# The last image of a windowed-attention block and dynamic convolution: early mean and taps, rows exchanged by channel group, two convolution pieces on TensorE and one on three engines

## The chip, the cores and the metric

The kernel runs on one core of one Trainium2 chip, as one launch. A core has five engines with instruction streams of their own: TensorE (matmul, PE in the profile), VectorE (DVE), ScalarE (ACT), GpSimd (POOL) and SyncE (SP), which here only issues DMAs. They meet through semaphores, and each takes its own instructions strictly in order. The metric is the device time of one execution in microseconds, lower is better. The kernel before takes 2823.23 us (median of three runs, 2822.96 to 2826.73).

## The reference

The input is 16 images of 192 channels and 56 x 56 pixels, float32. Two layers follow each other.

The first is a shifted-window attention block: layer norm over the channels, attention in 7 x 7 windows (shift 3, 6 heads) with relative position bias, a projection, a residual, a second layer norm, a two-layer network 192-768-192 with gelu, and a residual.

The second is the layer that the change touches, a depthwise convolution whose weights depend on the image:

```python
pooled = x.mean(axis=(2, 3))
t = pooled @ w1.T
t = gamma * (t - running_mean) * rsqrt(running_var + EPS) + beta
t = relu(t)
wt = t @ w2.T + b2            # 9 weights per channel and image
wt = wt * MASK                # of the 3 x 3 taps only the first four are left
out = depthwise_conv(x, wt, padding=1) + bias
```

The four taps left are the three of the row above and the left neighbour in the same row. Nothing of an image's convolution can be computed before the mean over all of its pixels is known, and the mean needs the end of the first layer.

## The kernel before

**Tiling.** An image is cut into four units of 14 rows. 64 partitions hold the channels of one group (`g`, three groups of 64), and the two halves of the partitions (`P(0)`, `P(1)`) hold two halves of the image, 28 rows each (`LR`), of which a unit has seven (`WS`) in each half; a unit has 392 pixels (`UT`) per half. The image lives in `xt[b % 3]`, 128 partitions x 3 groups x 29 rows x 56; row 0 is a copy of the neighbouring half's last row (the "halo"), which the tap above needs. There are 64 units (`S`); each goes through attention, projection, first layer (`first_layer`, L799, six chunks `f` into `hid`, with gelu on ScalarE, L811) and second layer (`second_layer`). Four units stand at different stages at the same time.

**Second layer.** `second_layer` goes over the three channel groups; for each it multiplies the six chunks of `hid` (128 hidden units x 2 halves x 392) with `wf2` into one bank of PSUM (L837, 12 matmuls a group). Then `ends` (L824, VectorE) adds bias and residual, writes the pixels back into `xt` and leaves their sum in `sums`.

**Taps.** After the fourth unit `taps(b)` reduces `sums` (L859), multiplies with `w1t` (L867, 6 matmuls), scales, applies relu and multiplies with `w2r` (L879 to L897, VectorE) into `wt`, the four weights per channel. Then it sends the two halo rows of all groups with two DMAs from SyncE (L903).

**Convolution.** `conv(b, i)` computes one of six pieces: half of the rows of each half image (`hf`) by channel group (`g`); a piece has 128 partitions x 14 rows x 56. ScalarE takes the tap straight above with the bias (L929), VectorE adds the other three with one multiply-add each (L953), ScalarE sets one row of the second half's piece anew (L946: the image row 0, which has no row above), and SyncE stores the piece in two or three DMAs (L966). For the first 15 images the pieces go through the tiles `yt` and lie beside the attention of the next image. For the last image nothing follows: its results are written into `hid`, whose chunk `i` becomes free when the second layer has read it.

**Order.** The kernel writes every operation into a plan (`Plan.add`) with an engine, an estimated duration, what it reads and writes, a lag, and a `slack`: how long after its place in TensorE's order it is due. `Plan.order` then simulates the engines with these estimates: TensorE keeps the order in which operations were added; every other engine takes, among the operations that are ready first, the one due first. The instructions are issued in the order that comes out, and each engine then runs its own in that order. For the last image the order that comes out takes the six pieces tap by tap on VectorE: all first taps, then the others; SyncE's queue holds the two halo DMAs and then the 15 stores.

The main loop (`for r in range(-2, S + 3)`) adds the operations of all stages of a step `r`. At the last step, `r = S + 2`, only the second layer of the last unit, the taps and the six pieces are left.

Of the kernel before, what the change touches and what calls it, by code (L numbers as in the profile page):

```python
# [45 lines left out]
class Plan:  # L46
# [7 lines left out]
    def add(self, eng, dur, fn, reads=(), writes=(), lag=0.0, slack=60.0, by=None):  # L54
        i = len(self.ops)
        deps = set()
        reads, writes = flat(reads), flat(writes)
        for k in reads:
            if k in self.writer:
                deps.add(self.writer[k])  # L60
        for k in writes:
            if k in self.writer:
                deps.add(self.writer[k])
            deps.update(self.readers.get(k, ()))
        for k in reads:
            self.readers.setdefault(k, []).append(i)
        for k in writes:
            self.writer[k] = i
            self.readers[k] = []
        deps.discard(i)  # L70
        self.ops.append((eng, dur, fn, sorted(deps), lag, slack, by))
# [70 lines left out]
def tile_swin_then_dynamic_conv(  # L142
# [37 lines left out]
    def sb(name, *shape):  # L180
        return const.tile(list(shape), F32, tag=name, name=name)
# [40 lines left out]
    m2 = sb("m2", 128, HT)  # L222
    rs = sb("rs", 128, HT)
    sums = [sb(f"sums{i}", 128, G, NU) for i in range(2)]
    pooled = sb("pooled", 128, G)
    trow = sb("trow", 128, RED)
    prod = sq.rearrange("p g t -> p (g t)")[:, 0 : G * NTAP * RED]
# [32 lines left out]
    def X(s):  # L260

        b, u = divmod(s, NU)
        return [("x", b % 3, u, i) for i in range(3)]
# [550 lines left out]

            add("ACT", 0.95, go, [pk, "b1f", "table"], [("hid", f)])

    def second_layer(s):
        b, u = divmod(s, NU)
        xv = rows(s).rearrange("p g r c -> p g (r c)")
        for g in range(G):  # L820
            p, pk = bank()

            def ends(p=p, g=g):
                nc.vector.scalar_tensor_tensor(  # L824
                    xv[:, g],
                    p[:, 0, 0:UT],
                    vecs[:, 5, g : g + 1],
                    xv[:, g],
                    ALU.add,
                    ALU.add,  # L830
                    accum_out=sums[b % 2][:, g, u : u + 1],
                )

            for f in range(NFC):
                def product(p=p, g=g, f=f):
                    for ab in range(2):
                        nc.tensor.matmul(  # L837
                            p[P(ab), 0, 0:UT],
                            wf2[:, f, g * 64 : (g + 1) * 64],
                            hid[:, f, ab],  # L840
                            start=(f == 0),
                            stop=(f == NFC - 1),
                            tile_position=(0, 64 * ab),
                        )

                add("PE", 0.66, product, [("hid", f), ("wf2", f // 2)], [pk])
                if f == NFC - 1:
                    add("DVE", 0.65, ends, [pk, "vecs"], X(s) + [("sums", b % 2)])


    def taps(b):


        p, pk = bank()
        sl = b % 3
        add(
            "DVE",
            0.2,
            lambda: nc.vector.tensor_reduce(pooled, sums[b % 2], AX.X, ALU.add),  # L859
            [("sums", b % 2)],  # L860
            ["pooled"],
        )

        def product():
            for g in range(G):
                for ab in range(2):
                    nc.tensor.matmul(  # L867
                        p[P(ab), 0, 0:RED],
                        pooled[:, g : g + 1].broadcast_to([128, 64]),
                        w1t[:, g],  # L870
                        start=(g == 0),
                        stop=(g == G - 1),
                        tile_position=(0, 64 * ab),
                    )

        add("PE", 0.3, product, ["pooled", "w1t"], [pk])

        def scale():
            nc.vector.tensor_tensor(trow, p[:, 0, 0:RED], bns, ALU.mult)  # L879
            nc.vector.tensor_tensor(trow, trow, bnb, ALU.add)  # L880
            nc.vector.scalar_tensor_tensor(
                prod,
                trow.rearrange("p (o r) -> p o r", o=1).broadcast_to([128, G * NTAP, RED]),
                0.0,
                w2r.rearrange("p g t r -> p (g t) r"),
                ALU.max,
                ALU.mult,
            )

        add("DVE", 1.2, scale, [pk, "bn", "w2r"], ["sq", "trow"])  # L890
        w = wt[b % 2].rearrange("p g t -> p (g t)")

        def fin():
            nc.vector.tensor_reduce(
                w.rearrange("p (k o) -> p k o", o=1), prod, AX.X, ALU.add
            )
            nc.vector.tensor_tensor(w, w, b2t.rearrange("p g t -> p (g t)"), ALU.add)  # L897

        add("DVE", 0.9, fin, ["sq", "b2t"], [("wt", b % 2)])
        t = xt[sl]  # L900
        for to, of, row in ((0, 1, LR), (1, 0, LR)):
            def go(to=to, of=of, row=row):
                nc.sync.dma_start(t[P(to), :, 0, :], t[P(of), :, row, :])  # L903
            add("SP", 0.65, go, X(b * NU + NU - 1), [("halo", sl, to)], lag=2.5)

    pieces = [(hf, g) for hf in range(2) for g in range(G)]

    def conv(b, i):
        hf, g = pieces[i]
        sl = b % 3  # L910
        yi = (b * 6 + i) % 2
        y, yk = yt[yi], ("y", yi)
        if b == B - 1:

            y = hid[:, i].rearrange("p a (r c) -> p (a r) c", c=IMG)
            yk = ("hid", i)
        nr = LR // 2
        src = xt[sl][:, g]
        prev = src[:, nr * hf : nr * hf + nr]
        same = src[:, nr * hf + 1 : nr * hf + nr + 1]  # L920
        w = wt[b % 2]
        keys = [k for u in range(NU) for k in X(b * NU + u) if u // 2 == hf or u == 2 * hf - 1]
        if hf == 0:
            keys += [("halo", sl, 0), ("halo", sl, 1)]
        keys.append(("wt", b % 2))
        add(
            "ACT",
            1.05,
            lambda: nc.scalar.activation(  # L929
                y, prev, AF.Identity, bias=vecs[:, 6, g : g + 1], scale=w[:, g, 1:2]  # L930
            ),
            keys + ["vecs"],
            [yk],
        )
        for t, dst, s_ in (
            (0, y[:, :, 1:], prev[:, :, : IMG - 1]),
            (2, y[:, :, : IMG - 1], prev[:, :, 1:]),
            (3, y[:, :, 1:], same[:, :, : IMG - 1]),
        ):
            if t == 3 and hf == 1:  # L940

                r = IMG - SHIFT - LR - nr
                add(
                    "ACT",
                    0.35,
                    lambda: nc.scalar.activation(  # L946
                        y[64:128, r], zero[64:128], AF.Identity, bias=vecs[64:128, 6, g : g + 1]
                    ),
                    ["vecs", "zero"],
                    [yk],  # L950
                )
            def go(t=t, dst=dst, s_=s_):
                nc.vector.scalar_tensor_tensor(  # L953
                    dst, s_, w[:, g, t : t + 1], dst, ALU.mult, ALU.add
                )
            add("DVE", 1.4, go, keys, [yk])
        ch = slice(g * 64, g * 64 + 64)
        parts = [(0, 0, nr, SHIFT + nr * hf)]
        first = SHIFT + LR + nr * hf
        n = min(nr, IMG - first)  # L960
        parts.append((1, 0, n, first))
        if n < nr:
            parts.append((1, n, nr, 0))
        for h, lo, hi, at in parts:
            def go(h=h, lo=lo, hi=hi, at=at):
                nc.sync.dma_start(out[b, ch, at : at + hi - lo, :], y[P(h), lo:hi])  # L966
            add("SP", 0.65, go, [yk], [], lag=12.0)

    def table(name):
        add("ACT", 1.3, lambda: nc.scalar.preload_act_table_set(name), [], ["table"])  # L970
# [411 lines left out]
    for r in range(-2, S + 3):  # L1382
# [43 lines left out]
            fold_proj()  # L1426
        if has(r):
            turn_shares()
        if has(r - 3):
            second_layer(r - 3)  # L1430
        b, k = divmod(r - 3, NU)
        weighing = k == NU - 1 and 0 <= b < B
        if has(r - 1):
            biased_rows(r - 1)
            for _ in projection(r - 1):
                if weighing:
                    taps(b)
            statistics(1, r - 1)
        elif weighing:
            taps(b)  # L1440
        if not early and has(r + 1):
            queries_keys(r + 1, (0, 1, 2))
        if has(r - 2):
# [5 lines left out]
        for b in range(B):  # L1449
            k = r - (b * NU + NU + 3)  # L1450
            if b == B - 1 and r == S + 2:
                for i in range(6):
                    conv(b, i)
            elif b < B - 1 and 0 <= k < 3:
                conv(b, 2 * k)
                conv(b, 2 * k + 1)
# [80 lines left out]
```

## Time and profile before

| | us |
|---|---|
| median of three runs | 2823.23 |
| the profiled execution, its own time | 2820.61 |
| its span, first to last instruction | 2818.8 |
| TensorE busy | 2754.4 (98%) |
| VectorE busy | 1833.4 (65%) |
| ScalarE busy | 1671.2 (59%) |
| GpSimd busy | 1570.5 (56%) |
| end of TensorE's last layer | 2789.0 |
| end of VectorE's last multiply-add | 2811.1 |

The profile is one execution. Each row of its tables names a line, an engine, an operation and tiles (out<-in), the shape, how many there were, the time they were busy and the mean of one. Rows marked "q" (SPq, ACTq) are the engine's instruction queue, here the issuing of DMAs. A matmul in float32 shows as two records. A timeline row gives start and duration in microseconds from the start of the span. Rows of stretches give length, then busy time and number of instructions of TensorE, its weight loads, VectorE, ScalarE and GpSimd, then the granted clock of TensorE (1.00 is full), the DMA share and GB/s.

### The profile page before, as it was taken

How to read it: one execution, taken by the hardware profiler on the slowest of the kernel's cores; microseconds unless marked ns; L12 is line 12 of the kernel's file. 1: busy time of each engine (PE TensorE's matmuls, PEld its weight loads, DVE VectorE, ACT ScalarE, POOL GpSimd, SP SyncE). 2: the span in 40 equal slices, each digit the busy share in tenths (PEclk: the TensorE clock that was granted, in tenths of full speed). 3: DMA queues.
4: the chain of work that ended last, by engine and by line, in shares of the span. 5: the costliest groups of instructions: out<-in, count | busy, mean ns of one | idle time of the engine just before them, and what ended most of it. 6: DMA issues, size and time to landing. Idle time of an engine off the chain costs nothing.

```text
span 2818.8 us, 79628 instructions
## 1 busy us (share of the span) xinstructions
PE 2754.4 (98%) x34337; PEld 1716.8 (61%) x34337; DVE 1833.4 (65%) x3321; ACT 1671.2 (59%) x2530; POOL 1570.5 (56%) x1424
## 2 busy tenths in 40 slices
PE   7899999999999999999999999999999999999995
PEld 5566666666666666566566666566666666666652
DVE  6565676667576675766757676675766757666663
ACT  3656656556566566566556566565665666565552
POOL 5565564565565565564665555555655655655530
PEclk9899999999999999999999999999999999999998
DMA  6312232223314223232233313233142243312131
GB/s 130 80 28 48 64 89 49 67 63 79 79 43 105 42 62 85 54 89 59 61 69 79 78 43 89 41 79 79 43 105 55 50 85 74 84 44 65 31 76 39
DMA packets 122232, 189.35 MB, mean 67 GB/s; under 512 B 31208, under 2 KB 96664, under 8 KB 121880
## 3 DMA queue, kind: packets, MB, share of 16 engines
q1 hardware_dynamic: 117512, 184.24, 29.3%
q8 instruction: 270, 4.42, 0.7%
q10 hardware_dynamic: 4368, 0.02, 0.1%
q14 instruction: 82, 0.67, 0.1%
HBM read 66.81 MB, written 38.98 MB: 38 GB/s over the span
## 4 chain that ended last, share of the span: by engine, by line
PE 96%; DVE 1%; ACT 1%; POOL 1%; issue 1%; DMA 0%; ACTq 0%; SPq 0%; DVEq 0%; POOLq 0%
PE ps L837 27%; PE ps L799 27%; PE ps L469 14%; PE ps L654 9%; PE ps L760 5%; PE ps L690 5%; PE ps L549 5%; PE ps L746 3%; PE ps L318 2%; DVE hid L953 0%; POOL xs L425 0%; PE ps L867 0%; ACT o L717 0%; PE ps L383 0%; DVE trow L880 0%
## 5 line engine op out<-in xcount | busy, mean ns | idle before, releaser
L837 PE MATMUL ps<-hid,wf 128*64 128x392 f32 x4608 | 773.4, 494 | 3.3 <-issue 2.5
L799 PE MATMUL ps<-xs,wf 64*128 64x392 f32 x4608 | 769.5, 489 | 0.0
L799 PEld LDWEIGHTS ps<-xs,wf 64*128 64x128 f32 x4608 | 445.9, 187 | 312.5 <-issue 0.9
L837 PEld LDWEIGHTS ps<-hid,wf 128*64 128x64 f32 x4608 | 327.8, 137 | 413.8 <-issue 381.4
L302 POOL TENSOR_TENSOR fold<-sq 128x392 f32<-128x392 f32 x128 | 131.3, 1026 | 700.1 <-PE ps L318 693.6
L811 ACT ACTIVATE hid<-ps,b1f 128x784 f32<-128x784 f32 x384 | 343.0, 912 | 146.2 <-PE ps L799 143.4
L590 POOL TENSOR_TENSOR e<-e,top 128x784 f32<-128x784 f32 x192 | 285.6, 1503 | 253.8 <-DVE top L585 253.8
L469 PE MATMUL ps<-xs,wqkv 64*128 64x392 f32 x2304 | 408.5, 504 | 11.0 <-POOL xs L436 9.7
L953 DVE SCALAR_TENSOR_TENSOR y<-x,wt,y 128x770 f32<-128x770 f32 x270 | 302.8, 1136 | 85.7 <-ACT y L946 63.3
L469 PEld LDWEIGHTS ps<-xs,wqkv 64*128 64x128 f32 x2304 | 220.3, 190 | 178.1 <-issue 21.8
L608 POOL TENSOR_TENSOR e<-e,tot 128x784 f32<-128x784 f32 x192 | 290.6, 1524 | 56.8 <-DVE tot L603 54.7
L654 PE MATMUL ps<-wqkv,xs 64*64 64x192 f32 x6144 | 278.1, 325 | 0.6 <-issue 0.4
L454 POOL TENSOR_TENSOR xs<-x,rb 128x392 f32<-128x392 f32 x192 | 249.6, 1328 | 25.4 <-DMA rb<-rsd 25.4
L575 DVE TENSOR_TENSOR e<-ps,bt 128x784 f32<-128x784 f32 x192 | 175.3, 968 | 130.2 <-PE ps L549 130.2
L717 ACT COPY o<-ps 32x392 f32<-32x392 f32 x512 | 246.5, 481 | 8.7 <-PE ps L690 2.3
L619 DVE STREAM_TRANSPOSE tt<-e 128x512 f32<-128x512 f32 x384 | 246.2, 685 | 5.8 <-POOL e L608 4.3
L654 PEld LDWEIGHTS ps<-wqkv,xs 64*64 64x64 f32 x6144 | 224.6, 133 | 35.1 <-issue 22.1
L482 ACT ACTIVATE q<-ps,qbs 128x400 f32<-128x400 f32 (+1 forms) x128 | 68.4, 589 | 288.2 <-PE ps L469 288.2
L602 DVE TENSOR_REDUCE tot<-e 128x16 f32<-128x784 f32 x192 | 182.1, 948 | 63.2 <-ACT e L597 63.1
L339 DVE TENSOR_TENSOR m<-ps,m 128x196 f32<-128x196 f32 (+1 forms) x64 | 23.2, 362 | 306.4 <-ACT m L332 306.3
L728 ACT ACTIVATE x<-x,pbt 128x392 f32<-128x392 f32 x192 | 105.4, 612 | 191.2 <-POOL xs L436 191.2
L666 ACT COPY v<-ps 128x768 f32<-128x768 f32 x128 | 102.3, 799 | 194.3 <-PE ps L654 194.3
(106 smaller groups left out, 3548.5 us busy)
## 6 DMA issues: line engine op xcount, KB each, us to landing
pt<-tt SPq DMA_DIRECT2D x256, 192.0 KB
x<-in_x_dram SPq DMA_DIRECT2D x112, 294.0 KB
out_dram<-y SPq DMA_DIRECT2D x135, 196.0 KB
pt<-tt SPq DMA_DIRECT2D x256, 96.0 KB
rb<-rsd SPq DMA_DIRECT2D x118, 196.0 KB
out_dram<-y SPq DMA_DIRECT2D x45, 154.0 KB
x<-in_x_dram SPq DMA_DIRECT2D x16, 168.0 KB
pt<-tt SPq DMA_DIRECT2D x128, 12.0 KB
```

The costliest lines, as they stand in the source:

```text
L454: nc.gpsimd.tensor_tensor(xs2[:, g], xv[:, g], rb[:, 1], ALU.mult)
L469: nc.tensor.matmul(p[:, ab, 0:UT], lhs_qk(ab, g, i), d[P(ab), g, 0:UT], start=(g == 0), stop=(g == G - 1), tile_position=(64 * ab, 0),)
L590: nc.gpsimd.tensor_tensor(ev, ev, top[j].broadcast_to([128, 16, N]), ALU.subtract)
L602: nc.vector.tensor_reduce(tot[j], ev, AX.X, ALU.add)
L608: nc.gpsimd.tensor_tensor(ev, ev, tot[j].broadcast_to([128, 16, N]), ALU.mult)
L619: nc.vector.transpose(tt[:, kb, 16 * j : 16 * j + 16], src)
L654: nc.tensor.matmul(p[P(w % 2), ab, i * DIM : (i + 1) * DIM], d[P(ab), g, w * N : w * N + 64], wqkv[P(ab), g, 2 * DIM :], start=(g == 0), s ...
L717: add("ACT", 0.5, lambda dst=dst, src=src: nc.scalar.copy(dst, src), [k], [("o", j, i)])
L799: nc.tensor.matmul(p[:, ab, 0:UT], wf1[P(ab), g, f * 128 : (f + 1) * 128], xs2[P(ab), g], start=(g == 0), stop=(g == G - 1), tile_position ...
L811: nc.scalar.activation(hid[:, f], p[:, :, 0:UT], AF.Gelu, bias=b1f[:, f : f + 1])
L837: nc.tensor.matmul(p[P(ab), 0, 0:UT], wf2[:, f, g * 64 : (g + 1) * 64], hid[:, f, ab], start=(f == 0), stop=(f == NFC - 1), tile_position= ...
L953: nc.vector.scalar_tensor_tensor(dst, s_, w[:, g, t : t + 1], dst, ALU.mult, ALU.add)
```

## The change

For the 15 images before the last nothing is computed in another way; `taps` is cut into `mean`, `taps` and `halos`, and the row-0 operation and the stores of `conv` become functions of their own (`first_row`, `stores`). For the last image:

- `early_mean`: the sum of the last unit's pixels is built before the second layer ends: the residual's sum (`xsum`, a VectorE reduction of the rows) plus `wf2` times the sums of `hid` over the pixels (`hsum`, six VectorE reductions; 18 matmuls with one column) plus the bias. The 18 matmuls stand after group 0 of the second layer.
- `taps` of the last image stands in the middle of group 1 (`amid`, after chunk 2).
- `halos` sends the rows of groups 0 and 1 when group 1 has ended (`("fin", 1)`), and those of group 2 when it has ended; four DMAs instead of two.
- `conv_product`: pieces 4 (second rows, group 1) and 2 (first rows, group 2) are computed on TensorE. GpSimd scales an identity matrix (made in `q2`) with the tap weights of the channels, four 128 x 128 matrices in `q128` and `kbd`; 8 matmuls (two blocks of seven rows, four taps) add the taps in PSUM; ScalarE moves the result into `hid` with the bias (0.95 planned) and issues the stores from its own queue.
- Piece 0 is shared by three engines: ScalarE forms two of the products in `yt`, GpSimd adds them, VectorE has the last tap.
- Pieces 3, 5 and 1 stay on ScalarE and VectorE. The pieces wait for single groups (`("fin", g)`), not for all rows.
- Planned durations, lags and slacks of the last image's operations differ (0.95 instead of 1.4 for a multiply-add, lag 4 instead of 12 for a store, slack 50 and 52 instead of 60).

In the order that comes out, VectorE has after the weights: the end of group 1, one multiply-add of piece 3, the end of group 2, six multiply-adds of pieces 3, 1 and 5, a 64 x 55 correction for piece 4, two multiply-adds, and the last tap of piece 0. ScalarE has the straight taps of pieces 3, 1 and 5, a row, the straight tap and the first product of piece 0, the move of piece 4, two rows, the second product of piece 0, three stores, the move of piece 2 and two stores. GpSimd has the eight scalings, then the two additions. SyncE has ten stores.

```diff
-    def second_layer(s):
+    def second_layer(s, groups=range(G), amid=None):
...
+                if amid is not None and f == 2:
+                    amid()
                 if f == NFC - 1:
-                    add("DVE", 0.65, ends, [pk, "vecs"], X(s) + [("sums", b % 2)])
+                    add("DVE", 0.65, ends, [pk, "vecs"], X(s) + [("sums", b % 2), ("fin", g)])
...
+    def early_mean(b):
...
+        for f in range(NFC):
+            add("DVE", 0.85,
+                lambda f=f: nc.vector.tensor_reduce(
+                    hsum[:, f : f + 1], hid[:, f].rearrange("p a t -> p (a t)"), AX.X, ALU.add
+                ),
...
+        add("DVE", 1.3, lambda: nc.vector.tensor_reduce(xsum, xv, AX.X, ALU.add), X(s), ["xsum"])
...
+        def product():
+            for g in range(G):
+                for f in range(NFC):
+                    nc.tensor.matmul(
+                        p[0:64, 0, g : g + 1],
+                        wf2[:, f, g * 64 : (g + 1) * 64],
+                        hsum[:, f : f + 1],
...
+    def halos(b, gs=slice(0, G)):
...
+                nc.sync.dma_start(t[P(to), gs, 0, :], t[P(of), gs, row, :])
...
+                X(b * NU + NU - 1) if b < B - 1 else [("fin", gs.stop - 1)],
...
+    def conv_product(b, i, unit, uk, room, dk):
...
+        for t in range(NTAP):
+            add("POOL", 0.35,
+                lambda t=t: nc.gpsimd.tensor_scalar(
+                    diag[:, t], unit, w[:, g, t : t + 1], None, ALU.mult
+                ),
...
+            for j in range(2):
...
+                    nc.tensor.matmul(
+                        dst, diag[:, t], s_, start=(k == 0), stop=(k == NTAP - 1),
...
+        add("PE", 5.3, product, keys, [pk])
...
+        stores(b, hf, g, y, yk, "ACT", 3.0)
...
-            add("DVE", 1.4, go, keys, [yk])
+            if not room or t == 3:
+                add("DVE", 0.95 if b == B - 1 else 1.4, go, keys, [yk])
+                continue
...
+                nc.scalar.activation(part, s_, AF.Copy, scale=w[:, g, t : t + 1])
+            add("ACT", 1.05, go, keys, part_keys)
...
+                nc.gpsimd.tensor_tensor(dst, dst, part, ALU.add)
+            add("POOL", 2.1, go, part_keys, [yk])
...
+        if r == S + 2:
+            ahead = early_mean(B - 1)
+            next(ahead)
+            second_layer(S - 1, (0,))
+            for _ in ahead:
+                pass
+            second_layer(S - 1, (1,), lambda: taps(B - 1))
+            halos(B - 1, slice(0, 2))
+            second_layer(S - 1, (2,))
+            halos(B - 1, slice(2, 3))
...
-                for i in range(6):
+                unit = q2.rearrange("p w b c -> p (w b c)")[:, 0:128]
...
+                conv_product(b, 4, unit, uk, room, [("q128", h) for h in range(2)])
...
+                conv_product(b, 2, unit, uk, room, [("kbd", h) for h in range(2)])
+                conv(b, 0, [(yt[i], [("y", i)]) for i in range(2)])
+                for i in (3, 5, 1):
                     conv(b, i)
```

## The prediction

> **What bounds the kernel now.** I read the page's shares first (TensorE 98% of the span, the last of 40 slices at half), then the chain of waits, then the timeline of the last 45 us. Up to 2789 us the chain is TensorE without gaps, and there both programs issue the same instructions in the same order on every engine. So only what follows the last `first_layer` can change, and the question is when the last store lands.
>
> ```profile
> 2776.93 12.07 PE L837 MATMUL ps<-hid,wf 128*64 128x392 f32 x72
> ...
> 2781.32 0.62 DVE L824 SCALAR_TENSOR_TENSOR x<-ps,vecs,x 128x392 f32<-128x392 f32 x1 [15.61 <-PE ps L837]
> ...
> 2793.14 5.70 ACT L929 ACTIVATE hid<-x,vecs,wt 128x784 f32<-128x784 f32 x6 [13.87 <-DVE wt L897]
> 2794.21 16.86 DVE L953 SCALAR_TENSOR_TENSOR hid<-x,wt,hid 128x770 f32<-128x770 f32 x18 [1.19 <-ACT hid L929]
> ...
> 2806.47 9.68 SPq L966 DMA_DIRECT2D out_dram<-hid  x15
> ```
>
> In this timeline (start, duration) TensorE ends its last layer at 2789.0; mean and taps take VectorE to 2793.0; then VectorE alone does 18 multiply-adds, 0.937 us apart, while TensorE and GpSimd have nothing. Also seen: VectorE idles 15.61 us before 2781.32.
>
> ```profile
> 2797.01 9.40 DVE hid L953 x10
> 2806.41 0.93 DVEq L1533
> 2807.34 3.73 DVE hid L953 x4
> ```
>
> The chain of waits ends on VectorE at 2811.07. The span ends later, at 2818.8: SyncE issues 15 stores, 0.645 us each and back to back, and ends 2.65 us after the last issue (2816.15). The stretches say what DMA does meanwhile (last three columns: TensorE clock, DMA share, GB/s):
>
> ```profile
> 2811.10:2816.20 5.10, 0.00 (x0) 0.00 (x0) 0.00 (x0) 0.00 (x0) 0.00 (x0) 0.50 0.81 245
> 2816.20:2818.80 2.60, 0.00 (x0) 0.00 (x0) 0.00 (x0) 0.00 (x0) 0.00 (x0) 0.50 0.32 97
> ```
>
> So the tail is 16.9 us of VectorE and a store queue that starts only when the first piece is whole, since the old order takes all pieces' taps in turn.
>
> **The change part by part**, on the old time axis.
>
> *Early mean.* Six reduces of `hid` on VectorE, 0.95 us each (128x784 reduces, L602: 948 ns), each after its gelu; the gelus end at 2768.1 to 2778.0, so the last reduce ends at 2779.0, inside the 15.61 us of idle time and 2 us before TensorE needs it. The row sum (128x1176, 1.45 us by the same rate) lies in the idle 12.55 us before 2754.8. Cost nothing; without that cover TensorE would wait out the last reduce.
>
> *The product with the sums* is new on TensorE, between groups 0 and 1 of the last layer: 18 fp32 matmuls of one column, 36 records. Rows for such records:
>
> ```profile
> 51.46 4.18 PE L1115 MATMUL ps<-vecs,wf 64*128 64x1 f32 x36
> ...
> 85.60 0.28 PE L1195 MATMUL ps<-bv,wp 128*64 128x1 f32 x2
> 85.80 0.27 PE L1199 MATMUL ps<-bv,wp 64*64 64x1 f32 x2
> 86.01 0.28 PE L1195 MATMUL ps<-bv,wp 128*64 128x1 f32 x2
> ```
>
> L1195 has the same 128x64 weights and one column: two records per 0.20 us, so 36 x 0.10 = 3.6 us, which I take. The ends: 2.0 us (L867, 12 records in 0.56 us, spread over two column halves: 0.057 each per half) and 4.0 us (L1115, 0.111 each).
>
> *The clock.* These columns stream almost nothing:
>
> ```profile
> 42.33:45.74 3.41, 1.92 (x12) 1.25 (x14) 2.51 (x3) 0.78 (x2) 3.33 (x5) 1.00 0.16 32
> ...
> 52.57:55.98 3.41, 3.41 (x30) 3.27 (x30) 3.31 (x7) 3.04 (x7) 2.56 (x3) 1.00 0.54 116
> 55.98:59.39 3.41, 3.41 (x14) 2.55 (x13) 2.48 (x6) 1.03 (x4) 2.71 (x3) 0.50 0.00 0
> 59.39:62.81 3.42, 3.42 (x84) 2.63 (x81) 2.67 (x6) 0.53 (x1) 0.00 (x0) 1.00 0.95 219
> 117.42:120.83 3.41, 1.10 (x34) 0.91 (x36) 3.31 (x7) 3.31 (x9) 3.41 (x4) 1.00 0.02 5
> 120.83:124.25 3.42, 3.42 (x24) 2.41 (x22) 1.67 (x3) 3.35 (x7) 2.71 (x3) 0.50 0.00 0
> ```
>
> A stretch of one-column matmuls (52.57 to 55.98) counts as busy throughout, yet the next 3.41 us have half the clock; 32% of real work (117.42) also lost it, 56% (42.33) kept it. The 3.6 us product leaves one such window near a third of real work. If the clock falls, 3.41 us at half rate lose at most 1.7 us, some 1.4 us where part of it lies in the product itself. I take 0.7, midway between 0 and 1.4. The Trainium skill, "TensorE: Matmul & The Clock Gate", Part 1, sets the clock by how busy TensorE was in a window of about 3.4 us; read by busy time it would charge nothing here, while the row at 52.57 charges the half clock.
>
> *Taps.* The product of L867 (0.5 us) stands in the middle of group 1: 2781.0 + 3.6 + 2.0 + 0.5 = 2787.1. The five VectorE steps from L879 to L897 took 2790.78 to 2793.02, 2.24 us: weights at 2789.5, 3.5 us earlier than now. The last two layer groups end at 2793.1, 4.1 us later than now.
>
> *Exchanged rows.* Four DMAs instead of two, two of them after group 1 alone. SyncE has nothing else queued. Before: issued at 2789.88, moving until 2792.2. After, the last pair is issued at 2794.7 and lands about 2797.0; its only user, the second TensorE piece, starts at 2798.3. Hidden.
>
> *Two pieces on TensorE.* Each has 8 matmuls of 128x128 weights, 16 records. L383 has that form, its records 0.327 us apart at full clock: 5.23 us. Twice that, at half clock throughout, would end at 2819, with no gain; but a window full of streaming brought the clock back each time (55.98, then 59.39), so I take 5.23. 2793.1 to 2798.3 to 2803.6. Eight GpSimd scalings of 128x128 make the weights; GpSimd has no such row. Between a fill of 128x196 (0.26 us) and the line through L436 and L425 (84 elements 0.366, 343 elements 1.00: 0.47) I take 0.4; GpSimd is idle then, and four are done by 2791.2: no cost. Each piece is moved out by ScalarE (0.91 us, as L811) and stored from ScalarE's queue: after the second, 2804.7 + 2 x 0.645 + 2.65 = 2808.7. The move of the first stands ahead of GpSimd's second addend in ScalarE's order, which therefore is ready only at 2801.2.
>
> *VectorE.* 18 multiply-adds become 10, a 64x55 correction, and two GpSimd adds of 128x770: 2.0 us each by L302 (392 elements in 1.03; the ends are 1.5, L590 with 784 elements and a broadcast operand, and 2.6, L454). Here GpSimd and VectorE meet:
>
> ```profile
> L880 DVE TENSOR_TENSOR trow<-trow,bnb x16: 209/1413/1435, 287.6 to 2791.0; 128x48 f32<-128x48 f32 x16
> ...
> L824 DVE SCALAR_TENSOR_TENSOR x<-ps,vecs,x x192: 534/626/628, 154.7 to 2789.2; 128x392 f32<-128x392 f32 x192
> ```
>
> L880 reads two SBUF tiles: 209 ns in the tail, where GpSimd is idle, about 1413 in the 15 images where GpSimd works. L824, one operand in PSUM, keeps its time. So the adds take VectorE's time too: I add them in line. The Trainium skill, "SBUF — State Buffer", "Who interferes with whom", says just this against the change: a two-SBUF-input VectorE instruction and a GpSimd instruction that reads SBUF exclude each other for the whole instruction; by it the adds stand in line, without it rival 1 holds.
>
> The path: the first piece may overwrite `hid` only after group 2's fourth step (2791.8), so ScalarE starts it then and VectorE's first multiply-add runs from 2793.0. Behind it waits the end of group 2 (0.63), to 2794.6. Six more at 0.93, to 2800.2; correction, 2800.4; first add, 2802.4; two multiply-adds, 2804.2; second add, 2806.2; the last, 2807.2. Three stores are left for SyncE: 2809.2, and 2.6 more: 2811.8. With 0.7 for the clock 2812.5, which is 6.3 us under 2818.8. The profiled execution took 2820.61 us, 1.8 more than its span and 2.6 under the median 2823.23; the same 6.3 from the median gives 2816.9.
>
> **The rivals.**
> 1. *The adds do not hold VectorE up.* Then the last multiply-add waits only for the second add (2801.2 + 2.0), and the end is 2809.4, or 2810.1 with the clock: 8.7 us saved, 2814.5. For it: median L953 of 1021 ns even in busy stretches. Against: its maximum, 2255, and L880.
> 2. *The one-column product is cheap* (2.0 us) and the clock holds: 1.6 + 0.7 better, span 2810.2, 2814.6. For it L867, against it L1195.
> 3. *Dear tail*: adds as slow as L454 (1.33 us per 392, so 2.6 each), or stores bound by data: 2.35 MB at 245 GB/s from 2801.5 on take 9.6 us, plus 1.5: 2812.6, 0.8 later. Together with a full clock loss, and scalings up to 0.8 us (see 4), 1 to 4 us saved: about 2821.
> 4. *Slower than before: the GpSimd scalings.* All eight stand ahead of both adds. About 3.5 us of them (0.44 each) fit ahead of VectorE's run; beyond that they exclude its multiply-adds as the adds do, and each us goes to the end. From (3.5 + 6.3) / 8 = 1.2 us each the change loses; at 1.5 the end is 2812.5 + 8.5 = 2821.0 and the time 2825.4. For it: the form has no row. Against it: all GpSimd rows up to 128 elements lie under 0.5 us.
>
> **How the numbers follow.** Chances: forecast 0.45 (own range 2815 to 2819: clock and product), rival 1 0.12, rival 2 0.23, rival 3 0.13, rival 4 0.07. 0.2% is 5.6 us, about what a measurement can tell. Of the forecast's cases 0.28 save more than that; with rivals 1 and 2 faster 0.63; the rest of the forecast and rival 3 give 0.30 within; slower 0.07. Rivals 1 and 2 together reach 11 us saved (2812); with 0.7 us for the spread of the median the low end is 2811.5. The high end, 2821.5, takes in most of rival 3.
>
> **What would show it.** Right: TensorE busy to about 2804; reduces of `hid` in the old idle time; weights at 2789 to 2790; GpSimd's adds in gaps of VectorE or multiply-adds stretched to 2 us; the last SyncE store issued about 2809.5. Wrong: VectorE waiting for the sums' product or for a TensorE piece, scalings over 0.5 us, or last stores on ScalarE's queue.

## The result and the profile after

The changed kernel takes 2817.17 us (median of 20 runs, 2807.56 to 2822.9) where the kernel before takes 2824.05 us (20 runs, 2816.99 to 2830.15): a ratio of 0.9974, 95% interval 0.9965 to 0.9982, so 5.1 to 9.9 us less. A second set, taken later, gives 2818.72 against 2824.19 us, ratio 0.9977 (0.9968 to 0.9986). Forecast were 2816.9 us, 6.3 less.

The two profiled executions hide this: 2820.74 us after (span 2818.9, granted clock 0.993) against 2820.61 before. The reason stands in the timeline, at the first matmul of the last `first_layer`. First a row of before, then the timeline of after from there on (start, duration, engine, line; in brackets the idle time before it and what ended it):

```profile
2764.88 12.12 PE L799 MATMUL ps<-xs,wf 64*128 64x392 f32 x72
```

```profile
2771.30 12.12 PE L801 MATMUL ps<-xs,wf 64*128 64x392 f32 x72
...
2784.42 0.97 DVE L874 TENSOR_REDUCE hsum<-hid 128x1 f32<-128x784 f32 x1 [1.00 <-ACT hid L813]
2787.36 2.15 PE L896 MATMUL ps<-hsum,wf 128*64 128x1 f32 x35
...
2789.60 0.15 DVE L909 TENSOR_TENSOR pooled<-pooled,ps 64x3 f32<-64x3 f32 x1 [1.32 <-PE ps L896]
2791.34 0.53 PE L921 MATMUL ps<-w1t,pooled 128*64 128x48 f32 x11
...
2794.05 0.17 DVE L951 TENSOR_TENSOR wt<-wt,b2t 128x12 f32<-128x12 f32 x1
...
2794.32 2.35 POOL L1013 TENSOR_SCALAR q<-q,wt 128x128 f32<-128x128 f32 x4 [23.57 <-DVE wt L951]
...
2794.80 5.66 SPq L961 DMA_DIRECT2D x<-x  x4
2796.66 3.15 POOL L1013 TENSOR_SCALAR kbd<-q,wt 128x128 f32<-128x128 f32 x4
...
2797.73 1.02 DVE L1114 SCALAR_TENSOR_TENSOR hid<-x,wt,hid 128x770 f32<-128x770 f32 x1 [2.96 <-ACT hid L1099]
2797.80 5.46 PE L1034 MATMUL ps<-x,q 128*128 128x392 f32 x16
...
2799.22 7.52 DVE L1114 SCALAR_TENSOR_TENSOR hid<-x,wt,hid 128x770 f32<-128x770 f32 x6
...
2802.79 2.19 POOL L1126 TENSOR_TENSOR hid<-hid,y 128x770 f32<-128x770 f32 x1 [2.99 <-ACT y L1123]
2803.10 5.36 PE L1034 MATMUL ps<-x,kbd 128*128 128x392 f32 x16
...
2805.93 2.24 POOL L1126 TENSOR_TENSOR hid<-hid,y 128x770 f32<-128x770 f32 x1 [0.94 <-ACT y L1123]
2806.76 8.56 SPq L997 DMA_DIRECT2D out_dram<-hid  x10
2806.77 1.47 DVE L1061 SCALAR_TENSOR_TENSOR hid<-x,wt,hid 64x55 f32<-64x55 f32 x1
2808.27 2.88 DVE L1114 SCALAR_TENSOR_TENSOR hid<-x,wt,hid 128x770 f32<-128x770 f32 x3
```

In these two executions the body, where both programs issue the same instructions, took 6.4 us longer after (2771.30 against 2764.88). That is scatter: in twelve profiles of kernels that all have the changed body, this matmul starts anywhere from 2764.3 to 2771.3 us. What follows it repeats to a few hundredths: the weights (L951) end 22.91 or 22.92 us later in every kernel that has the early mean and one product of sums. So from here on all times are counted from that matmul, and "the tail" is what lies between it and the end of the span:

| from the first matmul of the last `first_layer`, us | before | after |
|---|---|---|
| last layer group's matmuls end | 24.12 | 26.57 |
| the four weights ready | 28.14 | 22.92 |
| VectorE's first multiply-add starts | 29.33 | 26.43 |
| VectorE's last multiply-add ends | 46.18 | 39.85 |
| SyncE's last issue of a store ends | 51.27 | 44.01 |
| end of the span (the tail) | 53.94 | 47.65 |

6.3 us are gained, and all of them ahead of the last multiply-add (6.33 us). The column of before stands on one profile. From the last multiply-add to the end it took 7.76 us before and takes 7.80 after, though only four stores are then still to be issued, where before it was seven. The chain of waits of after still ends on VectorE, and the stretches say what comes behind it (stretch, length, then busy time and instructions of TensorE, weight loads, VectorE, ScalarE, GpSimd; last three the granted clock, the DMA share, GB/s):

```profile
2802.28 4.46 DVE hid L1114 x3
2806.73 0.03 issue
2806.77 1.47 DVE hid L1061
2808.24 1.05 DVEq L1714
2809.29 1.86 DVE hid L1114 x2
```

```profile
2805.00:2807.00 2.00, 2.00 (x7) 1.14 (x6) 1.97 (x3) 0.79 (x1) 1.07 (x1) 1.00 0.68 178
2807.00:2809.00 2.00, 1.46 (x5) 0.57 (x3) 1.97 (x2) 0.21 (x1) 1.17 (x1) 1.00 0.52 120
2809.00:2811.00 2.00, 0.00 (x0) 0.00 (x0) 2.00 (x3) 0.71 (x1) 0.00 (x0) 1.00 0.64 171
2811.00:2813.00 2.00, 0.00 (x0) 0.00 (x0) 0.15 (x1) 0.00 (x0) 0.00 (x0) 0.82 0.97 220
2813.00:2815.30 2.30, 0.00 (x0) 0.00 (x0) 0.00 (x0) 0.00 (x0) 0.00 (x0) 0.50 0.89 219
2815.30:2818.90 3.60, 0.00 (x0) 0.00 (x0) 0.00 (x0) 0.00 (x0) 0.00 (x0) 0.50 0.57 146
```

From 2811, about when the last multiply-add ends, the DMA share is 0.97 and then 0.89 and the rate stands at 220 GB/s, while from 2805 to 2811 the share lies between 0.52 and 0.68. Two of SyncE's ten issues lasted 1.25 and 1.53 us, the others 0.47 to 0.59 us.

The stretch from the end of the last multiply-add to the end of the span, before and then after, shows what was left to move:

```profile
2811.06:2818.80 7.74, 0.00 (x0) 0.00 (x0) 0.01 (x1) 0.00 (x0) 0.00 (x0) 0.50 0.65 196
2811.15:2818.90 7.75, 0.00 (x0) 0.00 (x0) 0.00 (x1) 0.00 (x0) 0.00 (x0) 0.57 0.77 187
```

196 GB/s over 7.74 us are 1.52 MB, 187 GB/s over 7.75 us are 1.45 MB. So of the last image's 2.41 MB nearly the same part was still to be moved when VectorE had done, although after has fewer stores left to issue; that fits two ends of equal length.

### The profile page after: what moved, and what is told of

Same layout as the page of the kernel before. It is cut to its first block, busy times and chain, and to the rows that moved or that the text cites. A ratio compares the mean times of both kernels' runs of the same rounds, so it can differ in the third digit from the quotient of the medians.

```text
span 2818.9 us, 79781 instructions
## 1 busy us (share of the span) xinstructions
PE 2769.0 (98%) x34405; PEld 1729.2 (61%) x34405; DVE 1839.4 (65%) x3324; ACT 1674.8 (59%) x2532; POOL 1582.4 (56%) x1436
## 4 chain that ended last, share of the span: by engine, by line
PE 95%; DVE 2%; issue 1%; ACT 1%; SPq 0%; DMA 0%; POOL 0%; ACTq 0%; DVEq 0%; POOLq 0%
PE ps L839 27%; PE ps L801 27%; PE ps L471 13%; PE ps L656 9%; PE ps L692 5%; PE ps L762 5%; PE ps L551 5%; PE ps L748 2%; PE ps L320 2%; DVE trow L934 0%; DVE hid L1114 0%; POOL xs L427 0%; DVE x L790 0%; DVE sq L935 0%; PE ps L921 0%
```

## The experiments

**The mean alone.** The tail of the change keeps the early mean and taps, but all six pieces go through ScalarE and VectorE:

```diff
-                conv_product(b, 4, ...)
-                conv_product(b, 2, ...)
-                conv(b, 0, [(yt[i], [("y", i)]) for i in range(2)])
-                for i in (3, 5, 1):
+                for i in range(6):
                     conv(b, i)
```

> The early mean, the taps in the middle of group 1 and the split row exchange stay; all six pieces of the last image are computed by ScalarE and VectorE again, 18 multiply-adds. I measure the tail: from the first matmul of the last first layer to the end of the span (before 53.9 us, changed kernel 47.6 us); the run's body before that point scatters by several us and is left out. Theory A (the end follows VectorE's path): weights ready at 22.9 us of the tail instead of 28.1, but the first multiply-add only at about 26.4, since the pieces overwrite hid; 17 more and the end of group 2 bring VectorE to about 44, and the 15 stores on one queue end 7.7 us later as before: tail 51 to 52. Theory B (a store queue and its data set the end, whatever VectorE does): the same 15 stores start when the first piece is whole, so about the same number; this run prices the mean alone, 2 to 3 us of the 6.3.

Measured: a tail of 51.43 us, 2.51 less than before. Weights at 22.92 and first multiply-add at 26.43 as in the full change, last multiply-add at 43.82.

**The pieces alone.** Mean and taps stand behind the whole second layer again, the pieces on TensorE and the shared one stay:

```diff
-            second_layer(S - 1, (0,))
...
-            second_layer(S - 1, (1,), lambda: taps(B - 1))
+            second_layer(S - 1, (0, 1))
             halos(B - 1, slice(0, 2))
             second_layer(S - 1, (2,))
             halos(B - 1, slice(2, 3))
+            mean(B - 1)
+            taps(B - 1)
```

> Mean and taps after the whole second layer, as in the kernel before; the two TensorE pieces, the shared piece and the split row exchange stay. Theory A: weights at 28.1 us of the tail; TensorE has nothing to do until the scaled matrices are there (four scalings of 0.6 us), so its pieces end near 41.5 and their last store near 47; VectorE starts 3 us later than in the changed kernel (29.3 instead of 26.4) and ends near 43: tail 50 to 51. Theory B: stores start 3 us later and the tail is 3 us longer, the same 50 to 51. If mean and pieces simply add, this run should give back 2 to 3 us against 47.6, and the clock of TensorE may fall to 0.5 while it waits, which would put the TensorE pieces last, tail 52 or more.

Measured: a tail of 50.74 us, 3.20 less than before. The timeline and two stretches of this kernel:

```profile
2797.06 7.36 PE L1034 MATMUL ps<-x,q 128*128 128x392 f32 x16 [3.69 <-POOL q L1013]
2804.26 5.36 PE L1034 MATMUL ps<-x,kbd 128*128 128x392 f32 x16
```

```profile
2794.09:2797.06 2.97, 0.00 (x1) 0.00 (x1) 1.71 (x4) 1.22 (x2) 1.24 (x3) 0.50 0.03 5
2797.06:2800.90 3.84, 3.84 (x6) 2.18 (x7) 3.77 (x4) 3.44 (x5) 3.84 (x4) 0.50 0.00 0
```

TensorE waits 3.69 us for the scaled matrices and loses its clock: the first piece takes 7.2 us to the start of the second, where it takes 5.3 after. The two halves give 2.51 + 3.20 = 5.71 us, together they give 6.29; 0.6 us come from having both. That the lost clock is the reason isn't shown. Most of the 0.6 lies ahead of VectorE's last multiply-add, which ends 3.50 us earlier here and 2.36 in the run before, but 6.33 in the full change; and VectorE waits for neither TensorE piece here. What its trace does show is that six of the eight scalings now lie beside multiply-adds: they take 1.06 to 1.38 us instead of 0.60, and three multiply-adds 1.13 us instead of 1.02. Behind VectorE's end the span takes 8.06 us instead of 7.80; there the late second piece, whose last two stores are issued after VectorE has ended, may count.

**The product of the sums twice.** It is computed a second time right behind the first:

```diff
-            for g in range(G):
+            for g in [g for _ in range(2) for g in range(G)]:
```

> The 18 one-column matmuls run twice (the second pass overwrites the first with the same numbers), 72 records instead of 36. At the 0.058 us per record of the changed kernel this is 4.2 us instead of 2.1. If a window of one-column records counts as idle for the clock, the granted clock falls to 0.50 for 3.4 us soon after, and the last layer's groups end 2.1 + 1.7 us later. If being busy is enough, the clock stays at 1.00 and they end 2.1 us later. The tail: theory A 49.7 with the clock held, 51.4 with it lost.

Measured: a tail of 51.37 us, 3.72 more than after; weights at 26.69, 3.77 later. Timeline and stretches of this kernel:

```profile
2786.66 4.25 PE L896 MATMUL ps<-hsum,wf 128*64 128x1 f32 x71
...
2790.83 3.59 PE L839 MATMUL ps<-hid,wf 128*64 128x392 f32 x11
```

```profile
2788.00:2791.43 3.43, 3.43 (x56) 3.23 (x57) 0.15 (x1) 0.00 (x0) 0.00 (x0) 1.00 0.02 5
2791.43:2794.85 3.42, 3.42 (x24) 2.45 (x21) 0.00 (x0) 0.00 (x0) 0.00 (x0) 0.50 0.00 0
2794.85:2798.00 3.15, 3.15 (x23) 2.09 (x22) 2.65 (x7) 0.00 (x0) 0.61 (x2) 1.00 0.00 0
```

4.25 us of one-column matmuls, in which TensorE is busy throughout, cost the clock for one stretch of 3.4 us. Of the 3.77 us, 2.1 are the second product and 1.7 the half clock: the price that the prediction had set for a full loss. One product (2.15 us) does not cost it: the clock stays at 1.00 in all ten profiles of kernels that have just one. The Trainium skill, "TensorE: Matmul & The Clock Gate", Part 1, sets the clock by how busy TensorE was; here, as in the prediction's row, busy time by the profile does not tell it, since 3.43 us of 3.43 were busy ahead of the loss. And a delay ahead of the weights reaches the end almost whole (3.72 of 3.77).

**Piece 0 not shared.** It goes through ScalarE and VectorE like the other three; GpSimd adds nothing:

```diff
-                conv(b, 0, [(yt[i], [("y", i)]) for i in range(2)])
-                for i in (3, 5, 1):
+                for i in (0, 3, 5, 1):
                     conv(b, i)
```

> Piece 0 goes back to ScalarE and VectorE; GpSimd has the eight scalings only, and VectorE 12 multiply-adds instead of 10 and two adds. The forecast's accounting (the adds exclude VectorE for their whole time, 2.2 us each): two adds out, two multiply-adds in, VectorE ends 4.4 - 1.9 = 2.5 us earlier or, if ScalarE's order sets it, no later than 39.9 us of the tail. Rival 1 (adds beside VectorE's work): VectorE ends 1.9 us later. For the end: theory A gives a tail of 45 to 47, theory B 47.6 less what the stores start earlier.

Measured: a tail of 47.47 us, as good as after (47.65); 2816.16 us in its one run. VectorE's last multiply-add ends 0.9 us earlier though it has two more of them, and hardly any of that reaches the end: two store issues again last 1.5 us each. The expected 2.5 us earlier was a miss; it charged the additions with 4.4 us, and the next run gives them 2.77 (2.77 less 1.87 for two more multiply-adds is 0.9). Sharing the piece buys nothing.

**Fills in place of the additions.** Each of GpSimd's two additions is replaced by three fills of a tile that nobody needs any more; piece 0 lacks two of its four taps:

```diff
-                nc.gpsimd.tensor_tensor(dst, dst, part, ALU.add)
+                for _ in range(3):
+                    nc.gpsimd.memset(part, 0.0)
```

> In place of each of GpSimd's two additions stand three fills of the addend tile, so two taps of piece 0 are missing in the output; the fills only write, take about 0.7 us each, 2.1 in all, as long as an addition, and stand at the same place with the same waits. If GpSimd holds VectorE up only while it reads (the Trainium skill, SBUF — State Buffer, Who interferes with whom), the multiply-add of 2.59 us and the correction of 1.47 us beside the additions take 1.02 and 0.3, and VectorE ends about 2.7 us earlier, less what ScalarE's order takes back. If any GpSimd work does it, both stay stretched by up to 0.7 us, one fill. By the theory that the stores' data sets the end, the tail becomes at most 1 us shorter than 47.6.

Measured: the last multiply-add ends 2.77 us earlier, the tail is 46.02 us, 1.63 less. The line of the multiply-adds in after and then in this kernel (least, median and longest in ns):

```profile
L1114 DVE SCALAR_TENSOR_TENSOR hid<-x,wt,hid x10: 1007/1018/2590, 2797.7 to 2810.1; 128x770 f32<-128x770 f32 x10
```

```profile
L1114 DVE SCALAR_TENSOR_TENSOR hid<-x,wt,hid x10: 1007/1014/1164, 2791.5 to 2801.1; 128x770 f32<-128x770 f32 x10
```

GpSimd is busy for 2.33 us in place of each addition, yet no multiply-add beside the fills is stretched (the longest, 1.16 us, lies beside a scaling, in both kernels); beside an addition one took 2.59 us and the small correction 1.47 us instead of 0.28. So it is not GpSimd at work that holds VectorE up, but GpSimd reading. That is what the Trainium skill, "SBUF — State Buffer", "Who interferes with whom", states of a VectorE instruction with two SBUF inputs; the runs agree. Of 2.77 us that VectorE gains, 1.14 do not reach the end; at most 1 us had been expected to reach it.

**Half the bytes in the last stores.** Every store of the last image writes only the first half of its rows (the other output rows are left out); the number of stores and everything ahead of them stay:

```diff
-                q.dma_start(out[b, ch, at : at + hi - lo, :], y[P(h), lo:hi])
+                n = hi - lo if b < B - 1 else (hi - lo + 1) // 2
+                q.dma_start(out[b, ch, at : at + n, :], y[P(h), lo : lo + n])
```

> Every store of the last image writes only the first half of its rows, so half of the last image's output is left out; the 15 DMAs, their queues and all computing stay. In the changed kernel SyncE's last issue ends 4.2 us after VectorE's last multiply-add, with two issues of 1.25 and 1.53 us, and the span ends 3.6 us after that. If the data of the stores sets the end (the stores wait for DMA engines that are 90 to 100% busy), the long issues go away, the last issue comes about 2 us after the last multiply-add and the tail falls from 47.6 to 44.5. If the issuing itself, or VectorE's path, sets it, the tail stays between 47 and 48.

Measured: a tail of 45.10 us, 2.55 less, with VectorE unchanged (39.84). The stretches around and behind the end of the last multiply-add (2804.15):

```profile
2803.00:2805.00 2.00, 0.00 (x0) 0.00 (x0) 1.15 (x2) 0.00 (x0) 0.00 (x0) 0.83 0.75 183
2805.00:2807.00 2.00, 0.00 (x0) 0.00 (x0) 0.00 (x0) 0.00 (x0) 0.00 (x0) 0.50 0.64 150
```

The DMA share falls to 0.64 to 0.75, no issue is long any more, and the last one ends 2.6 us after VectorE instead of 4.2. So the bytes of the stores set at least 2.55 us of the changed kernel's end: their number is the same here. The 5.3 us that are left behind VectorE are near what the forecast had for issues and landing alone (4.6).

**All stores from SyncE.** The five stores of the TensorE pieces go from ScalarE's queue to SyncE's:

```diff
-        stores(b, hf, g, y, yk, "ACT", 3.0)
+        stores(b, hf, g, y, yk, "SP", 3.0)
```

> The stores of the two TensorE pieces go back to SyncE's queue: 15 stores on one queue, in the order of the plan, where each waits for the one ahead. If the stores' data sets the end, the number of queues is worth little: tail 47 to 49, the loss coming from stores that wait behind a later piece. If issuing sets it, five more issues of 0.645 us make it 50 to 51.

Measured: a tail of 49.16 us, 1.5 more than after and between the two expectations. SyncE's first store goes out at 35.46, the first of ScalarE's would have at 33.06; so the second queue is worth 1.5 us. That it is so because bytes start earlier fits the runs with half the bytes and with early pieces, but this run alone doesn't show it.

**One store over both halves.** The rows that both halves of a piece have go out in one store over 128 partitions, 12 stores instead of 15, the same bytes:

```diff
+                dst = bass.AP(
+                    base.tensor,
+                    base.offset,
+                    [[LR * IMG, 2], [IMG * IMG, 64], [1, m * IMG]],
+                )
+                q.dma_start(dst, y[:, 0:m].rearrange("p r c -> p (r c)"))
```

> The changed kernel, but the rows that both halves of a piece have go out in one store over all 128 partitions (two blocks of 64 channels, 28 rows apart in the output) instead of two stores of 64 partitions: 12 stores instead of 15, the same bytes. What sets the rate of the last stores? If a store of one half is the limit (219 GB/s between 2813 and 2815.3 in the changed kernel, 346 GB/s in the best slice, where stores of both queues ran), the last 7.8 us shrink by up to 2 us: the end at 45.6 to 46.6 us from the first matmul of the last first layer, against 47.65. If the 16 DMA engines are what is full (share 0.89 to 0.97 then), only the number of issues counts and the end stays at 47.0 to 47.7. If such a store is spread over fewer engines because its outer step has only two entries, the DMA share falls far below 0.5 while stores run and the end comes 5 us or more later. The Trainium skill, "DMA: Bandwidth & Descriptors", says in the section on why a DMA increments its semaphore by 16 that the number of engines is the largest up to 16 that divides the slowest dimension of both patterns; read so, it would be two engines here.

Measured: a tail of 81.88 us, 34 more than after. Two of the stretches in which only stores run:

```profile
2825.00:2835.00 10.00, 0.00 (x0) 0.00 (x0) 0.00 (x0) 0.00 (x0) 0.00 (x0) 0.50 0.13 49
2835.00:2845.00 10.00, 0.00 (x0) 0.00 (x0) 0.00 (x0) 0.00 (x0) 0.00 (x0) 0.50 0.13 50
```

A DMA share of 0.13 is that of two engines of 16, and 50 GB/s would be 25 for each. The rule of the Trainium skill, "DMA: Bandwidth & Descriptors", in its section on why a DMA increments its semaphore by 16, which the expectation drew on, agrees with this. What holds the last stores of after at 220 GB/s therefore stays open: this form could not show it. A ceiling for stores of 64 partitions it is not, since the same stores ran at 245 GB/s in the kernel before (2811.10 to 2816.20).

**Pieces finished one after another.** Pieces 3, 1, 0 and 5 get tiles that are free early (`e_t` and `fold`) instead of `hid`, which the second layer holds to its end, and each is finished and stored before the next; no piece is shared:

```diff
+    spare = {3: (e_t[0]...), 1: (e_t[1]...), 5: (e_t[2]...), 0: (fold[:, 0]...)}
...
-            y = hid[:, i].rearrange("p a (r c) -> p (a r) c", c=IMG)
-            yk = ("hid", i)
+            place, yk = spare[i]
+            y = place.rearrange("p (r c) -> p r c", c=IMG)
...
-                conv(b, 0, [(yt[i], [("y", i)]) for i in range(2)])
-                for i in (3, 5, 1):
-                    conv(b, i)
+                for i, due in ((3, 20.0), (1, 26.0), (0, 32.0), (5, 38.0)):
+                    conv(b, i, due=due)
```

> Two things at once, both to start the stores earlier: the four pieces of ScalarE and VectorE go into tiles that are free by then (three softmax tiles and a statistics tile) instead of hid, so the first need not wait until the last layer has read hid; and they are finished one after the other (piece 3, 1, 0, 5) instead of tap by tap. Piece 0 is not shared with GpSimd, as in the run without sharing. If the stores' data sets the end: first SyncE store at 27 to 29 us of the tail instead of 35.5, stores spread over 12 us, end set by the last pieces: tail 42 to 44, and a ratio of 0.9955 to 0.996 to the kernel before. If VectorE's path sets it: its first multiply-add starts 2.3 us earlier and two more multiply-adds replace two adds, tail 44 to 46.

Measured: a tail of 43.85 us, 3.8 less than after and 10.1 less than before; 2813.94 us against 2822.32, ratio 0.9970 (0.9959 to 0.9981). Timeline:

```profile
2795.95 0.52 SPq L997 DMA_DIRECT2D out_dram<-e  x1
...
2797.80 3.03 SPq L997 DMA_DIRECT2D out_dram<-e  x4
...
2802.76 1.10 SPq L997 DMA_DIRECT2D out_dram<-fold  x2
...
2804.72 0.28 DVE L1061 SCALAR_TENSOR_TENSOR hid<-x,wt,hid 64x55 f32<-64x55 f32 x1
...
2805.09 1.02 DVE L1121 SCALAR_TENSOR_TENSOR e<-x,wt,e 128x770 f32<-128x770 f32 x1
2806.14 2.00 SPq L997 DMA_DIRECT2D out_dram<-e  x3
```

The first store goes out at 27.75 instead of 33.06, SyncE has issued seven before VectorE ends its last piece, and from the last multiply-add (37.91, 1.9 earlier than after) to the end it takes 5.9 us instead of 7.8. In this stretch 1.15 MB are moved (194 GB/s over 5.94 us), 1.45 in after. The expected ratio, 0.9955 to 0.996, was a little too good. The tiles, the order and the sharing changed together: how much each is worth isn't shown.

**The changed kernel and this one side by side**, both without edits:

> The changed kernel once more, beside the early-pieces kernel on the same chip. Counted from the first matmul of the last first layer, every theory expects the end at 47.6 us as in the first profile (47.65), since the tails of all runs repeat to a few hundredths of a us up to the stores. Time against the kernel before: 6 us less, a ratio of about 0.998.

> The kernel with the pieces finished one after another, once more and beside the changed kernel. If the end is set by the stores' data, which here begin 5 us earlier, the tail is again 43.9 us (43.85 in its first profile), 3.8 less than the changed kernel's, and the time 3 to 4 us below it, a ratio to the kernel before of about 0.9965. If the stores' data are not what counts and the first profile was lucky, the two kernels agree within 1 us.

Measured: tails of 47.62 and 43.84 us, as before to 0.03. Medians 2818.72 us (ratio 0.9977, 0.9968 to 0.9986) and 2815.48 us (0.9964, 0.9951 to 0.9978). The medians are 3.2 us apart, near the 3.8 of the tails; the intervals of the two ratios overlap, so the times alone would not yet tell the two apart. The tails do.

## Why the prediction was right, and where its steps were not

The forecast was an end 6.3 us earlier, 47.62 us on the axis used here; measured 47.65. What the change gains and where is as the prediction said. That the sum fits this closely is luck: terms that were too dear ahead of VectorE's end and one too cheap behind it cancel.

- *What can change.* Only what follows the last `first_layer`: right. The medians of the two sets differ by 6.9 and 5.5 us, the tails by 6.3.
- *Early mean at no cost.* Right: the last reduce ended at 2785.39, 2 us before the product began.
- *The product with the sums*: the forecast took 3.6 us, measured 2.15, the low end (0.058 us a record), which rival 2's row L867 gives. The prediction took the row that was like it in form (L1195, pairs of records that alternate with those of L1199) over the row that was a longer run (L867, 12 records); the new matmuls are a run too. Why the pairs are slower was not tried. The term was 1.5 us too large.
- *The clock.* 0.7 us were charged, the clock held: rival 2's second half. The upper bound was right, as the doubled product shows: a full loss costs 1.7 us.
- *Taps and layer groups.* Weights 5.2 us earlier than before where 3.5 had been said, the layer's end 2.4 later where 4.1 had been: both are 1.7 us off the forecast, of which the product makes 1.45.
- *Exchanged rows hidden*: right. The second pair was issued by 2800.46, the second TensorE piece starts at 2803.10, straight behind the first.
- *TensorE pieces*: right. 5.30 us from the first to the second, 5.23 said.
- *GpSimd's scalings*: 0.605 us each, not 0.4, above the row taken for 128 elements (0.47), and one that met a multiply-add took 1.41. Over 0.5 us was one of the prediction's signs of being wrong; it cost nearly nothing here, since TensorE starts its first piece as soon as the layer ends and one multiply-add was stretched by 0.15 us. All eight were done 5.6 us after the weights, so rival 4 (from 1.2 us each) was far.
- *The additions take VectorE's time*: right, and rival 1 false: with fills in their place VectorE ends earlier. But the price is 2.77 us, not 4.0: each addition (2.19 and 2.24 us) begins while a multiply-add that keeps its usual time still runs, by 0.50 and 0.80 us, and VectorE's next instruction is longer by 1.57 and 1.19 us, close to the rest. The forecast's pace held: where nothing is in the way, multiply-adds of 1.02 us start 0.93 us apart, as before. From the first multiply-add to the last 13.4 us, 14.2 said. Rival 1's own sum is off too: 2801.2 + 2.0, a last multiply-add of 1.0 and the forecast's 4.6 behind it make 2808.8, not 2809.4.
- *The end.* This is the step that failed most: "Three stores are left for SyncE: 2809.2, and 2.6 more", 4.6 us. It took 7.8. The forecast counted issues; what ran was bytes. Rival 3 had the mechanism, stores bound by data, with 0.8 us; it cost 3.2 over the forecast's term, and halving the bytes gave 2.55 back. The other 0.65 is mostly count: with half the bytes the last issue still ended 2.59 us after VectorE where 2.0 had been said, for four stores were left and not three. Rival 3's 2.35 MB are 2.41 (192 x 56 x 56 x 4 bytes), 0.2 us more at its rate, and its sum let the data run at 245 GB/s from the first store on. Measured were 0.52 to 0.68 of DMA share up to 2811, though: pieces that end together at the end leave the queue part empty ahead of it and full behind it.

In numbers from the first matmul: first multiply-add 1.7 us earlier than forecast, VectorE's run 0.8 shorter, 0.7 of clock not lost, together 3.2; the end 3.2 longer. Had the product been as dear as said, the tail would have been about 1.4 us longer and the gain 4.9, with the clock held (an estimate, from the doubled product, where a later start reached the end almost whole).

## What to carry to other kernels

When work at the end of a kernel gets shorter, price the last stores twice, by issues and by the bytes left when the last result is ready, and take the larger; pieces finished early, one after another, leave fewer bytes to the end (1.15 MB here) than pieces that all end together (1.45). Where the end of a run scatters by more than the change is worth, count from a fixed instruction just before the change: tails here repeat to a few hundredths of a microsecond (two pairs of profiles) while starts scatter by 7. Give GpSimd fills, or work that VectorE's two-input instructions don't meet; an addition on GpSimd beside them is paid for on VectorE too.

## What the runs showed of the hardware that was not expected

- The records of one-column fp32 matmuls with 128 x 64 weights (two a matmul) follow each other every 0.058 us in a stream. 2.15 us of them leave the clock at 1.00, while 4.25 us of them cost it for 3.4 us, though the profile shows TensorE busy throughout.
- SyncE's issues are no constant: in after most take 0.47 to 0.59 us, and 1.25 to 1.53 us where the DMA share comes near 1 (up to 1.8 us in the kernel with fills); at the end with half the bytes 0.55 to 0.65 again.
- Stores whose output pattern has an outer step of two ran at a DMA share of 0.13, that of two engines of 16, and 50 GB/s, though the tile has all 128 partitions.
- GpSimd scales a 128 x 128 float32 tile by a value per partition in 0.605 us and adds two of 128 x 770 in 2.2 us; beside a VectorE multiply-add the scaling took 1.41.
